# First tokens of the longer LSTMs in seven block products, and new places for the other stream's steps

## The chip, the cores and the metric

The kernel runs on one core of a Trainium2 chip. The time is the device time of one execution in microseconds (us), as a median over runs. The profile is one further execution, recorded instruction by instruction. TensorE is called PE here, VectorE DVE, ScalarE ACT, GpSimd POOL, and SyncE SP (in this kernel its queue issues nearly all DMAs). "L1155" is line 1155 of the kernel before.

## The reference, cut to what matters

Four residual layers work on x of 128 batches, 64 tokens and 256 channels in fp32. The change lies in layer 1: two graph convolutions, and then LSTMs over windows of p = 1, 2, 3 and 4 tokens, one after the other. Each overwrites the last token of each of its windows, so LSTM p+1 reads what LSTM p wrote.

```python
h = relu(adj @ (h @ Wg0 + bg0)); h = relu(adj @ (h @ Wg1 + bg1))
for p in range(1, 5):
    nw = 64 // p
    wins = h[:, :nw * p, :].reshape(128 * nw, p, 256)
    # per token: g = x_t @ Wih.T + h @ Whh.T + b; i, f, gg, o = split(g, 4)
    # c = sigmoid(f) * c + sigmoid(i) * tanh(gg); h = sigmoid(o) * tanh(c)
    last = lstm_last(Wih[p-1], Whh[p-1], bih[p-1], bhh[p-1], wins)
    h = h.at[:, arange(nw) * p + p - 1, :].set(last)
```

At a window's first token the state and the cell are zero. So only `x_t @ Wih.T` of the three gates i, gg and o is wanted there, and the cell is sigmoid(i) * tanh(gg).

## The kernel before, in words

**Tiling.** 512 rows of (batch, token) are a chunk; there are 16. Two chunks form a superchunk of 16 batches; there are eight, numbered 0 to 7. A superchunk lies in SBUF as `hT`: 128 partitions, two channel halves k, 64 tokens, 16 batches. The LSTM of p tokens has n = 16 * (64 // p) columns: 512, 336 and 256 for p = 2, 3, 4, and m = n/2.

**Seven block products.** A product of 256 by 256 weights with n columns is eight products of a 128x128 block with m columns. The kernel does it in seven (a Strassen-Winograd scheme). It needs sums of weight blocks, made once (`weight_sums`, L744) and reloaded per superchunk (`load_sets`, L883), sums of operands (`differences`, L309; `operands_x`, L1039, makes them for a token's input on POOL into an `xd` tile), and additions of the results. The class `Unit` (L1140) does this for one gate and one token. Kinds 1, 6, 7 and 4 fill bank x in turn, each on top of the last; kind 5 fills bank y; kinds 2 and 3 are two halves of bank z. Between them ACT copies a part out to `gates` (L1161) and DVE adds parts (L1164).

**The first token.** For p = 2, 3, 4 it is not done so. L1123 to L1128 are twelve plain products: three gates, two output halves, two input halves k, each n wide. Six with k = 0 come first, then a `yield`, then six with k = 1. ACT applies tanh or sigmoid straight from the banks (L1113), DVE makes the cell (L1119) and the state (L1093, `new_state`), and the operand sums of the state follow (`dh`, L313 to L316). Then come x products of token 1 for gates i and gg (kinds 5, 3 and 2: six of m columns), a `yield`, and token 1.

**Two streams.** All engines' queues are written in the order of the program. The LSTMs are a generator. Each `yield` is a mark n, counted from 0 in each superchunk; `yield "a"` is a half mark. In a superchunk the one-token LSTM ends at mark 3 and the others at 7, 13 and 21. At each mark the loop at the end runs the steps of the other stream due there, and they stand in every engine's queue at that place. Tuples name the marks:

- `convolutions` (15 steps a chunk) makes the next superchunk's `hT`: scaling; transposes and a trip through DRAM, with the load of xs; an addition (L284); statistics (L159, L160); two applies on ACT (L196); an aggregate on PE (L214); copies (L1005); products v (L915); bound (L921); products u (L929); bias (L935); a second aggregate; two ACT steps. `BEGUN` gives the first steps, a superchunk ahead, and `CONV` the rest (`FIRST` in superchunk 0).
- `residual` (three steps) puts the previous superchunk's `hT` back: transposes (L1277), loads, addition. Its tuple is `RESIDUAL`.
- `ahead` (six steps) prepares layer 2: a store and a reordering load, statistics, two applies, and transposes with a store (L272). Its tuples are `AHEAD` and `LATE`, and `FINAL` in the last superchunk.

Superchunk 7 has no convolutions. There `keep_busy` puts PE transposes at marks 5, 7, 9, 13 and 15.

**The end of an LSTM.** At its last token `new_state` writes `hT` in parts, the second channel half last (L1099; L1356 in the one-token LSTM), and then `ending` makes the operand sums for the next LSTM's token 1.

## Time and profile before

| what | value |
|---|---|
| time, median of 10 runs | 1877.54 us (1875.88 to 1879.07) |
| profiled execution, its own time | 1878.6 us |
| span in the profile, first to last instruction | 1876.8 us |
| mean granted PE clock | 0.998 of full |
| LSTM superchunks, first one-token product to the end of the last LSTM | 274 to some 1496 us |
| superchunk 3: LSTMs of 1, 2, 3, 4 tokens | 18.0, 42.7, 44.7, 49.2 us |
| PE idle in these | 0, 0, 0, 1.13 us |
| DVE busy in these | 13.2, 26.7, 29.5, 33.8 us |
| ACT busy in these | 14.9, 20.3, 25.3, 26.1 us |
| superchunk 7, the same four LSTMs | 18.0, 37.0, 43.9, 37.4 us |
| PE idle in these | 0, 0, 1.46, 1.87 us |

The page has parts: each engine's busy time, the span in slices, the DMA queues, the chain of work that ended last, and groups of instructions. A group has line, engine, operation, the names out<-in with shapes, a count, and then busy us and mean ns of one. The timeline lists instructions with start and duration in us; equal ones that follow each other are merged, and a bracket gives the idle time before and what ended it. A wide product appears as two passes, so the 288 products of L1126 count as 576.

### The profile page before, as it was taken

The page shows a single profiled execution, that of the slowest core. Times are in us where ns is not written, and L with a number is a line of the kernel's source. Part 1 is how long each engine was busy: PE and PEld are TensorE (multiplying, and loading weights), DVE is VectorE, ACT ScalarE, POOL GpSimd, SP SyncE. Part 2 cuts the span into 40 slices and gives each one's busy share as a digit, 9 for nine tenths or more (in the row PEclk, how much of TensorE's full clock was granted, in tenths as well). Part 3 has the DMA queues.
Part 4 walks back from the last instruction along what each step waited for, and adds up shares of the span by engine and source line. Part 5 has one row for each costly group of instructions (what it writes and reads, how often), then busy time and mean ns, then how long its engine had stood idle before and what let it go on. Part 6 is the DMA issues. An engine that isn't in the chain of part 4 may idle for free.

```text
span 1876.8 us, 39077 instructions
## 1 busy us (share of the span) xinstructions
PE 1848.0 (98%) x15077; PEld 1477.8 (79%) x15077; DVE 1245.2 (66%) x3150; ACT 1013.4 (54%) x2284; POOL 549.4 (29%) x704
## 2 busy tenths in 40 slices
PE   8999999999999999999999999999999999999998
PEld 6877856895897798699589689778968967777776
DVE  6768855566577666666666766666565567777776
ACT  5766635556456456555555645555565544444453
POOL 5855722122222212212222212222132113332232
PEclk9999999999999999999999999999999999999999
DMA  3223652134334433332433443343144254454433
GB/s 115 71 69 144 238 197 90 68 130 152 107 130 147 146 141 129 112 138 95 147 119 134 162 137 130 130 128 125 63 141 133 80 154 139 140 154 139 144 113 114
DMA packets 111274, 241.45 MB, mean 129 GB/s; under 512 B 11505, under 2 KB 74865, under 8 KB 111089
## 3 DMA queue, kind: packets, MB, share of 16 engines
q1 hardware_dynamic: 110192, 237.09, 37.5%
q8 instruction: 119, 1.95, 0.4%
q0 software_dynamic: 320, 1.05, 0.2%
q10 hardware_dynamic: 576, 0.82, 0.1%
q14 instruction: 67, 0.54, 0.1%
HBM read 170.50 MB, written 68.42 MB: 127 GB/s over the span
## 4 chain that ended last, share of the span: by engine, by line
PE 87%; DVE 6%; ACT 2%; DMA 2%; issue 1%; POOL 1%; SPq 0%; DVEq 0%; ACTq 0%
PE x L1155 21%; PE z L1155 10%; PE g L1126 9%; PE y L1155 5%; PE v L1580 5%; PE x L1340 4%; PE y L1340 3%; PE v L915 3%; PE u L929 3%; PE p_q L1587 3%; PE X L1776 3%; PE X L423 2%; PE X L499 2%; PE Y L1776 1%; PE Y L423 1%
## 5 line engine op out<-in xcount | busy, mean ns | idle before, releaser
L1155 PE MATMUL x<-xd,wset 128*128 128x128 f32 (+2 forms) x1152 | 256.9, 305 | 8.6 <-DVE gates L1164 8.5
L1155 PE MATMUL x<-hd,wset 128*128 128x128 f32 (+2 forms) x1152 | 255.3, 303 | 0.0
L1221 POOL TENSOR_TENSOR gates<-gates 128x512 f32<-128x512 f32 (+2 forms) x48 | 75.1, 1565 | 534.6 <-ACT gates L1084 534.6
L1084 ACT ACTIVATE gates<-gates,bias 128x256 f32<-128x256 f32 (+4 forms) x384 | 172.5, 488 | 103.7 <-DVE gates L1164 103.7
L1164 DVE TENSOR_TENSOR gates<-gates,x 128x128 f32<-128x128 f32 (+2 forms) x384 | 120.5, 321 | 145.2 <-PE x L1155 142.0
L1164 DVE TENSOR_TENSOR gates<-gates,z 128x128 f32<-128x128 f32 (+2 forms) x384 | 102.4, 318 | 150.2 <-PE z L1155 150.0
L1155 PEld LDWEIGHTS x<-xd,wset 128*128 128x128 f32 x1152 | 188.3, 192 | 16.6 <-DVE gates L1164 11.6
L1155 PEld LDWEIGHTS x<-hd,wset 128*128 128x128 f32 x1152 | 188.5, 192 | 5.0
L1126 PE MATMUL g<-hT,wset 128*128 128x256 f32 (+2 forms) x576 | 184.1, 474 | 0.1
L1126 PEld LDWEIGHTS g<-hT,wset 128*128 128x128 f32 x576 | 108.6, 190 | 68.1 <-issue 37.8
L1161 ACT COPY gates<-y 128x128 f32<-128x128 f32 (+2 forms) x192 | 53.9, 292 | 197.7 <-PE y L1155 195.9
L1155 PE MATMUL z<-hT,wset 128*128 128x128 f32 (+2 forms) x768 | 146.7, 303 | 0.0
L1155 PE MATMUL z<-hs,wset 128*128 128x128 f32 (+2 forms) x768 | 146.5, 303 | 0.2 <-DVE hs L1093 0.2
L1155 PEld LDWEIGHTS z<-hT,wset 128*128 128x128 f32 x768 | 117.2, 191 | 3.7
L1155 PEld LDWEIGHTS z<-hs,wset 128*128 128x128 f32 x768 | 117.2, 191 | 3.7 <-DVE hs L1093 0.3
L1113 ACT ACTIVATE gates<-g,bias 128x512 f32<-128x512 f32 (+2 forms) x144 | 74.9, 559 | 38.1 <-PE g L1126 37.5
L1084 ACT ACTIVATE gates<-x,bias 128x128 f32<-128x128 f32 (+2 forms) x192 | 74.8, 390 | 30.0 <-PE x L1155 27.6
L1155 PE MATMUL x<-hT,wset 128*128 128x128 f32 (+2 forms) x384 | 86.0, 306 | 0.2 <-ACT gates L1084 0.2
L1155 PE MATMUL x<-hs,wset 128*128 128x128 f32 (+2 forms) x384 | 84.9, 303 | 0.0
L1236 ACT ACTIVATE gates<-cell 128x256 f32<-128x256 f32 (+2 forms) x144 | 55.2, 383 | 48.4 <-DVE cell L1235 48.3
L1155 PE MATMUL y<-hd,wset 128*128 128x128 f32 (+2 forms) x384 | 79.7, 310 | 0.0
L1155 PE MATMUL y<-xd,wset 128*128 128x128 f32 (+2 forms) x384 | 77.5, 304 | 1.9 <-ACT gates L1113 1.9
(326 smaller groups left out, 4121.3 us busy)
## 6 DMA issues: line engine op xcount, KB each, us to landing
wset<-wfar SPq DMA_DIRECT2D x96, 960.0 KB, 6.5
hT<-far_h SPq DMA_DIRECT2D x124, 128.0 KB, 3.2
far_h<-hm SPq DMA_DIRECT2D x16, 512.0 KB, 2.8
far_n<-xs SPq DMA_DIRECT2D x16, 512.0 KB, 3.4
xs<-far_n SPq DMA_DIRECT2D x64, 128.0 KB, 4.1
far_x<-xs SPq DMA_DIRECT2D x16, 512.0 KB, 3.0
x<-far_x SPq DMA_DIRECT2D x64, 128.0 KB, 3.2
xt<-in_x_dram SPq DMA_DIRECT2D x15, 512.0 KB, 4.0
```

The lines of the kernel that those rows point to most:

```text
L423: nc.tensor.matmul(self.banks[tag][:, i * CH // 2 : (i + 1) * CH // 2], w, self.at[kind], start=first and not i, stop=True, skip_group_che ...
L915: nc.tensor.matmul(banks[m], wg0_sb[:, k, m * P : (m + 1) * P], agg[:, k, :], start=(k == 0), stop=(k == KD - 1))
L929: nc.tensor.matmul(banks[j // 2][:, j % 2, :], v[:, k, j * P : (j + 1) * P], wg1_sb[:, k, :], start=(k == 0), stop=(k == KD - 1))
L1084: nc.scalar.activation(gate(q, c, part), src, AF.Tanh if q == 2 else AF.Sigmoid, bias=bs[:, q * KD + c : q * KD + c + 1])
L1113: nc.scalar.activation(columns_of(gate(q, c)), natural(banks[q, c][:, :n].rearrange("p (w b) -> p w b", b=nb)), AF.Tanh if q == 2 else AF. ...
L1126: nc.tensor.matmul(banks[q, c][:, :n].rearrange("p (w b) -> p w b", b=nb), wsets[p, q][:, 2 * k + c, :], hv[:, k, : (nw - 1) * p + 1 : p, ...
L1155: nc.tensor.matmul(folded(self.psum(kind)), wsets[p, self.q][:, BLOCKS[kind][i], :], (ox[self.s] if part == "x" else oh)[kind], start=firs ...
L1164: nc.vector.tensor_add(gate(self.q, *dst), gate(self.q, *a), self.psum(kind))
L1221: nc.gpsimd.tensor_mul(gates[:, 0, :, :n], gates[:, 0, :, :n], gates[:, 2, :, :n])
L1340: nc.tensor.matmul(folded(ps(g, kind)), wih1[:, g, KINDS1[kind], :], right[kind], start=kind in (2, 5, 1), stop=True, skip_group_check=True)
L1580: nc.tensor.matmul(ps[:, i, :], hT[:, k, j, :], w[:, k, first : first + D], start=(k == 0), stop=(k == KD - 1))
L1776: nc.tensor.matmul(st[c, tag][:, i * CH // 2 : (i + 1) * CH // 2].rearrange("p (a n) -> p a n", n=P), w, st[c, "o7"][kind], start=first an ...
```

## The change

The first token of the two-, three- and four-token LSTMs becomes 21 products of m columns (class `First`): seven kinds for three gates. Copies, additions and acts come between them, and the biases stay in the acts. Gates i and gg take a bank of y and one of z each, gate o both of x. The marks within the first token change: the `yield` comes after kinds 1 and 5, and there is a new half mark (4.5, 8.5, 14.5) between the first and the second half of the state. Of token 1's x products only kinds 3 and 2 stay before the `yield`; kind 5 goes behind it. The input sums of the first token are made as well, so `xd` has three buffers. The weight set loses the one block that only the plain products used (15 to 14), and is stored in three pieces. The tuples of marks change. Without its empty lines, the diff is:

```diff
@@ -752,9 +752,9 @@
             for dst, a, b, op in ((4, 1, 3, OP.add), (5, 4, 0, OP.subtract), (6, 0, 1, OP.subtract),
                                   (7, 2, 5, OP.subtract)):
                 nc.gpsimd.tensor_tensor(v[:, :, dst], v[:, :, a], v[:, :, b], op)
-            far = dram.tile([P, 15, P], F32, tag=f"ws{p}{q}", name=f"wfar_{p}_{q}", bufs=1)
-            nc.sync.dma_start(far[:, :9], w[:, :9])
-            nc.sync.dma_start(far[:, 9:], w[:, 10:])
+            far = dram.tile([P, 14, P], F32, tag=f"ws{p}{q}", name=f"wfar_{p}_{q}", bufs=1)
+            for at, n, src in ((0, 1, 0), (1, 7, 2), (8, 6, 10)):
+                nc.sync.dma_start(far[:, at : at + n], w[:, src : src + n])
             wfar[p, q] = far
             yield
@@ -883,7 +883,7 @@
     def load_sets(n):
         for _ in range(min(n, len(coming))):
             p, q = coming.pop(0)
-            wsets[p, q] = w1.tile([P, 15, P], F32, tag="wset", name=f"wset_{p}_{q}", bufs=6)
+            wsets[p, q] = w1.tile([P, 14, P], F32, tag="wset", name=f"wset_{p}_{q}", bufs=6)
             nc.sync.dma_start(wsets[p, q], wfar[p, q])
@@ -1021,7 +1021,7 @@
-    BLOCKS = {1: (0, 8), 2: (2, 9), 3: (7, 14), 4: (3, 10), 5: (4, 11), 6: (5, 12), 7: (6, 13)}
+    BLOCKS = {1: (0, 7), 2: (1, 8), 3: (6, 13), 4: (2, 9), 5: (3, 10), 6: (4, 11), 7: (5, 12)}
     def columns_x(p, hv):
         nw, nb = hv.shape[2] // p, hv.shape[3]
@@ -1040,14 +1040,14 @@
         nw, nb, inner, tokens = columns_x(p, hv)
         m = nw * nb // 2
-        t = l1.tile([P, 7 * (T // 3) * NB], F32, tag="xd", name=f"xd_{name}_{s}", bufs=2)
+        t = l1.tile([P, 2 * CH], F32, tag="xd", name=f"xd_{name}_{s}", bufs=3)
         t = [t[:, i * m : (i + 1) * m].rearrange("p (a b) -> p a b", b=inner) for i in range(4)]
         b = {(k, j): tokens(k, s, j) for k in range(KD) for j in range(2)}
         for f in differences(nc.gpsimd, t, b[0, 0], b[0, 1], b[1, 0], b[1, 1]):
             f()
         return {5: t[0], 6: t[1], 7: t[2], 4: t[3], 1: b[0, 0], 2: b[1, 0], 3: b[1, 1]}
-    def lstm(p, hv, name, follows, x1, ending):
+    def lstm(p, hv, name, follows, ox, ending):
         nw, nb, inner, tokens = columns_x(p, hv)
@@ -1103,37 +1103,51 @@
         dh = differences(nc.vector, [hd[:, i, :m] for i in range(4)], b[0, 0], b[0, 1], b[1, 0], b[1, 1])
         oh = {i: folded(a) for i, a in {1: b[0, 0], 2: b[1, 0], 3: b[1, 1], 4: hd[:, 3, :m],
                                         5: hd[:, 0, :m], 6: hd[:, 1, :m], 7: hd[:, 2, :m]}.items()}
-        ox = {1: x1}
-
-        banks = {(q, c): bank(f"g{q}_{name}_{c}", tag) for q, tag in ((0, "y"), (2, "z"), (3, "x"))
-                 for c in range(KD)}
-        def first_acts(*qs):
-            for q in qs:
-                for c in range(KD):
-                    nc.scalar.activation(
-                        columns_of(gate(q, c)),
-                        natural(banks[q, c][:, :n].rearrange("p (w b) -> p w b", b=nb)),
-                        AF.Tanh if q == 2 else AF.Sigmoid, bias=bs[:, q * KD + c : q * KD + c + 1])
-
-        def first_cell(c):
-            nc.vector.tensor_mul(cells[:, c, :n], gate(0, c), gate(2, c))
-            nc.scalar.activation(gate(2, c), cells[:, c, :n], AF.Tanh)
-
-        products = [(q, c, k) for k in range(KD) for q in GATES[:3] for c in range(KD)]
-        for at, (q, c, k) in enumerate(products):
-            if at == 6:
-                yield
-            nc.tensor.matmul(
-                banks[q, c][:, :n].rearrange("p (w b) -> p w b", b=nb), wsets[p, q][:, 2 * k + c, :],
-                hv[:, k, : (nw - 1) * p + 1 : p, :], start=(k == 0), stop=(k == KD - 1))
-        first_acts(0, 2)
-        first_cell(0)
-        first_acts(3)
-        first_cell(1)
-        for c in range(KD):
-            new_state(0, c, every)
-            if not c:
-                dh[0]()
+
+        class First:
+
+            def __init__(self, q, tags):
+                self.q, self.ps = q, [bank(f"{t}{q}_{name}_{i}", t) for i, t in enumerate(tags)]
+
+            def psum(self, kind):
+                return self.ps[kind in (5, 3)][:, m:n] if kind in (2, 3) else self.ps[kind in (5, 3)][:, :m]
+
+            def product(self, kind):
+                nc.tensor.matmul(folded(self.psum(kind)), wsets[p, self.q][:, BLOCKS[kind][0], :], ox[0][kind],
+                                 start=kind in (1, 5), stop=True, skip_group_check=True)
+
+            def copy(self, c, j, kind):
+                nc.scalar.copy(gate(self.q, c, halves[j]), self.psum(kind))
+
+            def add(self, dst, a, kind):
+                nc.vector.tensor_add(gate(self.q, dst[0], halves[dst[1]]),
+                                     gate(self.q, a[0], halves[a[1]]), self.psum(kind))
+
+        firsts = [First(q, tags) for q, tags in ((0, "yz"), (2, "yz"), (3, "xx"))]
+
+        def all_first(*fs):
+            for f in fs:
+                for u in firsts:
+                    f(u)
+
+        def made(kind):
+            return lambda u: u.product(kind)
+
+        all_first(made(1), lambda u: u.copy(0, 0, 1), made(5), lambda u: u.copy(1, 1, 5))
+        yield
+        all_first(made(2), lambda u: u.add((0, 0), (0, 0), 2), made(3), made(6), lambda u: u.add((0, 1), (1, 1), 6),
+                  made(7), lambda u: u.add((1, 1), (1, 1), 7), lambda u: u.add((0, 1), (0, 1), 3), made(4),
+                  lambda u: act(u.q, 0, every, gate(u.q, 0)))
+        nc.vector.tensor_mul(cells[:, 0, :n], gate(0, 0), gate(2, 0))
+        nc.scalar.activation(gate(2, 0), cells[:, 0, :n], AF.Tanh)
+        all_first(lambda u: act(u.q, 1, halves[1], gate(u.q, 1, halves[1])),
+                  lambda u: act(u.q, 1, halves[0], u.psum(4)))
+        new_state(0, 0, every)
+        dh[0]()
+        yield "a"
+        nc.vector.tensor_mul(cells[:, 1, :n], gate(0, 1), gate(2, 1))
+        nc.scalar.activation(gate(2, 1), cells[:, 1, :n], AF.Tanh)
+        new_state(0, 1, every)
         dh[1]()
         dh[2]()
@@ -1201,14 +1215,14 @@
             return lambda u: getattr(u, f)(*a)
         A = [Unit(q, 1) for q in (0, 2)]
-        each(A, pe(5, "x"), pe(3, "x"), pe(2, "x"))
+        each(A, pe(3, "x"), pe(2, "x"))
         yield
         for s in range(1, p):
             last = s == p - 1
             B = [Unit(q, s) for q in (1, 3)]
             if not last:
                 ox[s + 1] = operands_x(p, hv, name, s + 1)
-            each(A, pe(5, "h"), do("copy", 5), pe(1), do("copy", 1), pe(3, "h"), pe(2, "h"), pe(6), do("u4"),
+            each(A, pe(5, "h" if s > 1 else "xh"), do("copy", 5), pe(1), do("copy", 1), pe(3, "h"), pe(2, "h"), pe(6), do("u4"),
                  do("c11"), do("c12"))
             each(B[:1], pe(5), do("copy", 5))
             each(A, pe(7), do("c22"), do("act", 0))
@@ -1301,9 +1315,8 @@
         t = []
         for i in range(2):
-            part = l1.tile([P, 7 * (T // 3) * NB], F32, tag="xd", name=f"xd_{name}_{i}", bufs=2)
-            for a in range(0, 2 * CH, CH):
-                v = part[:, a : a + CH]
+            part = l1.tile([P, 2 * CH], F32, tag="xd", name=f"xd_{name}_{i}", bufs=3)
+            for v in (part[:, :CH], part[:, CH:]):
                 wide = b[0, 0].shape[1:]
                 t.append(v.rearrange("p (a b) -> p a b", b=wide[1]) if len(wide) > 1 else v)
         a = b[0, 0], b[0, 1], b[1, 0], b[1, 1]
@@ -1420,7 +1433,7 @@
         def ending(p):
             if p < SKIP:
-                operands[p + 1] = operands_x(p + 1, hv, names[p + 1], 1)
+                operands[p + 1] = {s: operands_x(p + 1, hv, names[p + 1], s) for s in range(2)}
             elif sc < NCH // SUP - 1:
                 nxt = hTs[sc + 1].rearrange("p k (t b) -> p k t b", t=T)
                 operands[1] = block_sums(blocks(sc + 1, nxt), f"{sc + 1}_1")
@@ -1482,14 +1495,14 @@
-    RESIDUAL = (0, 3, 4), (2, 5, 5.5)
-    CONV = (3, 4, 4, 5, 5.5, 7, 8, 9, 10, 10), (3, 4, 4, 11, 11.5, 13, 14, 15, 15.5, 17, 18, 20)
-    BEGUN = (11, 11, 13, 14, 16), (17, 17.5, 19)
-    FIRST = (1, 2, 3, 3, 4, 4, 5, 5.5, 7, 8, 9, 10, 10), (3, 3, 5.5, 7, 8, 8, 11, 11.5, 13, 14, 15, 15.5, 17, 18, 20)
-    AHEAD = (4, 5, 7, 12, 14, 15), (6, 7)
-    LATE = 5, 6, 8, 9
+    RESIDUAL = (0, 3, 5.5), (2, 5, 8.5)
+    CONV = (3, 4, 5, 5.5, 7, 8, 9, 10, 10), (5, 6, 9.5, 11, 11.5, 13, 14, 15, 15.5, 17, 18, 20)
+    BEGUN = (11, 11, 14.5, 17, 19, 21), (17.5, 19, 21)
+    FIRST = (1, 2, 3, 3, 4, 4, 5, 5.5, 7, 8, 9, 10, 10), (1, 2, 4.5, 5, 6, 9.5, 11, 11.5, 13, 14, 15, 15.5, 17, 18, 20)
+    AHEAD = (6, 7), (9, 10)
+    LATE = (4.5, 5.5, 9, 9.5), (9, 11, 12, 19.5)
     IDLE = {5: 4, 7: 18, 9: 10, 13: 14, 15: 8}
-    FINAL = (4, 5, 10, 12, 12, 14), (6, 7, 11, 14, 14, 16)
+    FINAL = (6, 7, 11, 12, 15, 15.5), (9, 10, 15, 16, 17, 17.5)
     START = (0, 1, 0, 0, 0, 1, 0, 1, 1, 0, 0, 1, 1, 0, 1, 2, 2)
     tc.no_sync_barrier()
@@ -1526,8 +1539,6 @@
                     todo.setdefault(n, []).append(unit)
-            if sc > 1:
-                units(LATE[:1], aheads[sc * SUP - 3])
             if sc < last:
                 for i in range(SUP):
                     units((CONV if sc else FIRST)[i], convs[(sc + 1) * SUP + i])
@@ -1538,7 +1549,8 @@
             else:
                 units([0], convs[1])
             if sc > 1:
-                units(LATE[1:], aheads[sc * SUP - 3])
+                for i in range(SUP):
+                    units(LATE[i], aheads[(sc - 2) * SUP + i])
             if sc:
                 for i in range(SUP):
                     units((FINAL if sc == last else AHEAD)[i], aheads[(sc - 1) * SUP + i])
```

## The prediction

> **What bounds the kernel now.** I read the page first: busy shares, then the chain of work that ended last.

> ```profile
> PE 1848.0 (98%) x15077; PEld 1477.8 (79%) x15077; DVE 1245.2 (66%) x3150; ACT 1013.4 (54%) x2284; POOL 549.4 (29%) x704
> PE 87%; DVE 6%; ACT 2%; DMA 2%; issue 1%; POOL 1%; SPq 0%; DVEq 0%; ACTq 0%
> ```

> TensorE (PE) is the bound: it idles for 29 us of 1876.8. A product saved is time saved, if PE has no new wait; a wait of PE costs its whole length. So everything below is counted on PE's queue. What does one product cost? The groups of instructions, shapes kept apart (busy us, mean ns), show each fp32 product as two passes:

> ```profile
> L1126 PE MATMUL g<-hT,wset 128*128 128x512 f32 x192 | 85.6, 596 | 0.0
> L1126 PE MATMUL g<-hT,wset 128*128 128x336 f32 x192 | 55.6, 447 | 0.0
> L1126 PE MATMUL g<-hT,wset 128*128 128x256 f32 x192 | 42.9, 380 | 0.1
> ```

> The mean is a latency. From start to start, passes that follow each other in the timeline are 0.429, 0.283, 0.216 us apart at 512, 336, 256 columns, and in the blocked products of L1155 0.216, 0.143, 0.112 us at 256, 168, 128: half the columns, about half the time. Then I read the timeline at the three first tokens of one superchunk (start, duration), here the three-token LSTM, PE alone:

> ```profile
> 801.19 6.94 PE L1126 MATMUL g<-hT,wset 128*128 128x336 f32 x24
> 807.97 0.73 PE L1155 MATMUL y<-xd,wset 128*128 128x168 f32 x4
> 808.54 1.30 PE L1155 MATMUL z<-hT,wset 128*128 128x168 f32 x8
> 809.77 1.16 PE L214 MATMUL agg_c<-adjt_bd,cv 64*64 64x64 f32 x64
> ```

> No gap: the x products and the other stream's L214 hide the gates' chain (acts, cell, state, L313), and token 1 follows at 810.87. Last, PE's longer gaps in this stage. A recurring one:

> ```profile
> 885.88 1.29 DVE L284 TENSOR_TENSOR xs<-xs,cv 128x512 f32<-128x512 f32 x2 [1.11 <-DMA xs<-in_x_dram]
> 887.43 0.49 PE L1155 MATMUL x<-xd,wset 128*128 128x128 f32 x2 [0.90 <-DVE gates L1164]
> ```

> VectorE (DVE) stands in its queue before a DMA, and PE behind it. Such gaps are 0.64, 1.30, 1.06, 2.74 us in superchunks 0, 2, 3, 5 (5.7 us); one of 0.40 us at 40 to 50% of the four-token LSTM comes in superchunks 0 to 5.

> [...] L1356 takes 0.68 us, but 1.19 us where POOL's L314 runs. [...]

> **The change, part by part.**

> *Products.* Per superchunk 12 of n columns go, 24 x (0.429+0.283+0.216) = 22.3 us; 21 of n/2 come, 42 x (0.216+0.143+0.112) = 19.8 us. That is 2.5 us, over 8 superchunks 19.9 us, if nothing waits.

> *DVE, ACT, POOL, DMA work.* Per LSTM 12 adds (steps 0.33, 0.24, 0.20 us): 9 us more of DVE per superchunk of some 155 us, of which it is busy 103. ACT: six copies, and nine acts for six, about 7 us more. POOL: four differences more, 0.4 to 0.7 us each. None is PE time; they cost only where PE stands behind one, which the walks below count. Weight sets shrink from 960 to 896 KB; they land some 15 to 40 us before use. Twelve more DMA issues in the weight stage lie behind PE's work there: nothing. SP's moved puts stand before weight loads with that same slack: nothing; without it, up to the landing of 6.5 us once per LSTM. The third xd buffer adds no wait.

> *Two-token LSTM (T=758.54, PE's first product).* Its last operand comes late:

> ```profile
> 758.54 5.31 PE L1126 MATMUL g<-hT,wset 128*128 128x512 f32 x12
> 761.42 1.19 DVE L1356 TENSOR_TENSOR hT<-cell,gates 128x512 f32<-128x512 f32 x1 [0.17 <-ACT gates L1353]
> ```

> Before, six wide products covered it. After: L214 is moved ahead (1.1 us), six narrow products (2.6) end at T+3.7; the copies into the gates start only after the state at T+4.07, copy 0.37 and 0.2 of handing over, so product 2 starts at T+4.63: 0.9 us of PE wait. Fifteen products (6.5), four x products (1.7), L915 (3.4) and the two x products moved behind it (0.9) bring T+17.1. Before, 776.15-758.54 = 17.6. **-0.5 us.** L915 is the cover here: the bank that token 1 needs is free 3.9 us after product 4, at T+15.0, against T+16.3.

> *Three-token LSTM (T=801.19).* State at T+1.27, so product 2 waits 0.1. Product 7 waits for DVE's add of 6, and 4 for that of 7: product to add 0.55, add 0.33, back 0.16, against three products of 0.29: 0.17 each. Product 4 ends at T+6.45; x products 1.15 and L214 1.1: PE is at token 1 at T+8.7. Token 1's first bank is the one that product 4 filled, and ACT reads it only fourth after the tanh of cell 0: product 4 + 3.2 = T+9.65, with the way back T+9.75. That is 1.05 us, because only L214 (not a long L915 or L929) lies there. With the moved x products (0.57) T+10.3, against 9.7: +0.6. Behind it the h products wait 0.2 for the second state, since a residual sum (1.2 us of DVE) now stands ahead of it at mark 8.5. From superchunk 2 on 2.1 us of statistics at mark 9 stand ahead of token 1's adds (before: squares of 1.4): 0.6. **+0.8, from superchunk 2 on +1.4 us.**

> *Four-token LSTM (T=845.90).* 21 products 4.7, adds' pace 0.26 twice, x products 0.9, L929 3.45, moved x products 0.45: T+10.02 against 9.98. **0.0.** L929 covers the chain; without it the bank comes 2.8 us after product 4 and 1.9 us show. At marks 17 and 19 the moved statistics (2.1) and transposes (1.4) cost PE 0.2 each: **+0.4** in superchunks 0 to 5.

> *What the moves take away.* The conv input loaded at 17.5 and added at 19 is now loaded at 19 and added at 21: the DMA gap goes, 5.7 us; the apply at 16 goes, and with it 0.40 six times, 2.4 us.

> *First superchunk.* The aggregate at mark 4 waits for both applies: +1.0 in the two-token LSTM; the 1.27 us that acts of the three-token LSTM stood behind an apply go. With the rest 0.0.

> *Last superchunk.* No other stream covers, only short idle transposes, and its two-token LSTM waits still longer for its operand:

> ```profile
> 1381.47 1.19 DVE L1356 TENSOR_TENSOR hT<-cell,gates 128x512 f32<-128x512 f32 x1 [0.16 <-ACT gates L1353]
> ```

> From T=1377.72: state at T+4.94, product 2 at 5.5, product 4 ends at 12.0, bank at 15.9, moved x products: 16.7 against 13.3, +3.4. Three tokens: state T+2.67, product 4 at 7.8, bank 11.1: 11.7 against 9.7, +2.0. Four: +0.9. Gaps of 1.46 and 0.91 behind misplaced steps go: **+3.9 us.**

> *Sum.* Superchunks 2 to 6: 5 x (-0.5+1.4+0.0) + 4 x 0.4 - 5.1 - 1.6 = -0.6; superchunk 1: -0.5+0.8+0.4-0.4 = +0.3; 0: 0.0; 7: +3.9. Together some +4 us: a span of 1881, a run of 1882.5 beside the profiled one (1878.6, 1.8 above its span and 1.1 above the median), against the median **1882 us**. So of 19.9 us nothing is left; some 32 us of first-token waits and work behind take it, less 8 us of waits removed.

> **Rivals.**
> *Faster, 1869.* The one mechanism: the y bank in the three-token LSTM. If ACT frees it 1.1 us earlier, and DVE's statistics end in time, 1.85 us go from seven superchunks, 13 us. For it: ACT is only 57% busy in that LSTM (25.3 of 44.7 us). Against: the four acts and the tanh stand in a fixed order.
> *No change, 1878.* The last superchunk costs nothing net: its cover is short, but so were the gaps there.
> *Much slower, 1892.* DVE falls behind: marks 4.5, 8.5, 14.5 put 1.3 to 2.1 us before the second cell, and each of 24 first tokens loses 0.4 us more. Against: DVE is idle a third of the stage.
> That the change doesn't do what it says is excluded: the built program's queue has 21 products per first token.

> **How the numbers follow.** Forecast 0.38, faster 0.25, no change 0.25, much slower 0.12. Within 0.2% (3.8 us, about what a measurement of this kernel can tell from no change) is the third; slower is forecast and last, 0.50. Unknown in size are the bank-grained waits: from nothing (two bank waits gone, -13) to half a microsecond more at each first token (+12). Range 1868 to 1893; the forecast's own is 1879 to 1887.

> **What would show it.** Right: a PE gap of about 1 us before the first y product of token 1 in the three-token LSTM, put down to ACT; 0.9 us before product 2 in the two-token one; the L284 DMA gap gone; a last superchunk longer by 4 us. Wrong: first tokens without gaps (then 2.5 us per superchunk are gained), or gaps where the moved steps stand instead.

## The result, and the profile after

The changed kernel takes **1896.66 us** (median, 1895.88 to 1897.86), against 1877.64 before (median of 28 runs): a ratio of 1.0102, 95% interval 1.0093 to 1.0111. The forecast was 1882 us, with a range of 1868 to 1893. It is slower, as forecast, but by 19 us where 4 were counted, and outside the range.

The page of the kernel after, engine totals and the chain of work that ended last:

```profile
PE 1838.8 (97%) x15509; PEld 1513.8 (80%) x15509; DVE 1325.1 (70%) x3438; ACT 1053.2 (56%) x2500; POOL 599.1 (32%) x800
PE 79%; DVE 11%; ACT 5%; issue 2%; POOL 2%; DMA 1%; SPq 0%; ACTq 0%; DVEq 0%; POOLq 0%
```

PE was busy for 1848.0 of 1876.8 us; now it is for 1838.8 of 1895.7. The products did become cheaper, and PE's idle time went from 29 to 57 us. On the chain, DVE and ACT have 16% where they had 8% before. DVE works 80 us more; 9 us of that per superchunk are the additions that were counted.

So the question is where PE stands. The groups of instructions, shapes kept apart for the first line (busy us, mean ns, then PE's idle time ahead of the group and what ended it), give two places at once:

```profile
L1116 PE MATMUL y<-hT,wset 128*128 128x256 f32 x64 | 17.9, 402 | 4.8 <-ACT gates L1120 4.8
L1169 PE MATMUL x<-xd,wset 128*128 128x128 f32 (+2 forms) x1152 | 256.6, 304 | 12.3 <-ACT gates L1175 10.1
```

L1116 is the first token's product (L1120 its copy), and that wait was foreseen. L1169 is the later tokens' product (L1155 before), L1175 their copy (L1161 before). Its group stood for 8.6 us before, behind DVE. Now ACT's copies hold it for 10.1 us, and no step of the prediction has that.

The stretches of the timeline, from the first product of an LSTM to the first of the next (for the very last one, to its last product), say in which superchunk and LSTM the time lies (us; superchunk 4 is a typical one):

| | before | after | predicted | measured |
|---|---|---|---|---|
| up to the first superchunk | 274.0 | 274.7 | 0 | +0.7 |
| superchunk 0 | 157.98 | 160.80 | 0.0 | +2.8 |
| superchunk 1 | 153.71 | 155.01 | +0.3 | +1.3 |
| superchunks 2 to 6, sum | 774.0 | 776.2 | -0.6 | +2.1 |
| of these, superchunk 4: p = 1 and 2 | 60.68 | 60.27 | -0.5 | -0.4 |
| p = 3 | 44.71 | 45.96 | +1.4 | +1.25 |
| p = 4 | 48.30 | 49.24 | 0.0 | +0.9 |
| superchunk 7 | 146.33 | 153.33 | +3.9 | +7.0 |
| after the last LSTM | 370.8 | 375.8 | 0 | +5.0 |

The measured column adds up to 18.9 us, the difference of the spans. (The last LSTM of the kernel before ends at 1506.0 us. The table ahead of the prediction stopped at 1496, so it gives its four-token LSTM 10 us too little.)

The four waits that make up most of it, each in its timeline (start, duration; the bracket is the idle time ahead). First the four-token LSTM of superchunk 4, before the last token, DVE, ACT and PE together:

```profile
1045.95 0.15 DVE L194 SCALAR_TENSOR_TENSOR nmr_b<-mv_b,rstd_b 128x4 f32<-128x4 f32 x1
1046.14 1.09 ACT L196 ACTIVATE cv<-xs,nmr_b,rstd_b 128x256 f32<-128x256 f32 x2 [1.09 <-DVE nmr_b L194]
1047.14 0.41 ACT L1175 COPY gates<-y 128x128 f32<-128x128 f32 x2
1047.86 0.35 PE L1169 MATMUL x<-xd,wset 128*128 128x128 f32 x1 [1.40 <-ACT gates L1175]
```

The moved apply (L196, mark 19) stands at the head of ACT's queue. It waits for a small DVE operation (L194), which stands behind the end of the token before. The copies of the last token stand behind the apply, and PE behind the copies. From start to start PE loses 1.56 us here, in superchunks 0 to 4 alike, and 1.91 us in superchunk 5: 9.7 us.

Second, the two-token LSTM of superchunk 0:

```profile
296.78 0.23 POOL L99 TENSOR_SCALAR rstd_b<-mv_b 128x4 f32<-128x4 f32 x1 [4.23 <-DVE mv_b L160]
297.10 1.04 POOL L100 TENSOR_TENSOR rstd_b<-rstd_b,mhalf 128x4 f32<-128x4 f32 x1
298.11 0.95 POOL L313 TENSOR_TENSOR xd<-hT 128x256 f32<-128x256 f32 x1
299.11 1.00 PE L1116 MATMUL z<-xd,wset 128*128 128x256 f32 x2 [2.25 <-POOL xd L313]
```

Product 5 of the first token needs POOL's difference of the operand. POOL had stood idle for 4.23 us, waiting for DVE's statistics (L160): the square root of the other stream that needs them (L99, L100) stands ahead of the difference in POOL's queue. Before, the first token read the plain operand and needed no POOL.

Third, after the last LSTM, SP's queue (its DMA issues) and then PE:

```profile
1488.36 27.16 SPq L247 DMA_DIRECT2D far_n<-nm  x3
1515.58 0.42 SPq L1581 DMA_DIRECT2D wqv_sb<-wqv_far  x1
...
1522.43 1.96 PE L1599 MATMUL p_q<-hT,wqv_sb 128*128 128x512 f32 x4 [2.21 <-DMA wqv_sb<-wqv_far]
```

The weights of the next stage are issued at 1515.58 because three stores stand ahead, the last of them in place at mark 19.5. Before, that load was issued at 1478.6, 27 us ahead of its use. PE loses 2.4 us from start to start.

Fourth, what was predicted: a wait of 0.88 us in the three-token LSTM, before token 1, behind ACT (L1084), and one of 0.72 us from start to start before product 2 in the two-token one (0.56 us in the bracket), behind ACT's copy out of the other half of its bank (L1120):

```profile
923.61 0.65 ACT L1120 COPY gates<-y 128x256 f32<-128x256 f32 x2 [1.39 <-DVE hT L1369]
924.03 1.13 PE L1116 MATMUL y<-hT,wset 128*128 128x256 f32 x4 [0.56 <-ACT gates L1120]
...
969.37 1.16 PE L214 MATMUL agg_c<-adjt_bd,cv 64*64 64x64 f32 x64
971.41 0.52 PE L1169 MATMUL y<-xd,wset 128*128 128x168 f32 x2 [0.88 <-ACT gates L1084]
```

### The profile page after: what moved, and what is told of

Its sections match the earlier page's. It is cut to its first block, busy times and chain, and to the rows that moved or that the text cites. A ratio compares the mean times of both kernels' runs of the same rounds, so it can differ in the third digit from the quotient of the medians.

```text
span 1895.7 us, 40708 instructions
## 1 busy us (share of the span) xinstructions
PE 1838.8 (97%) x15509; PEld 1513.8 (80%) x15509; DVE 1325.1 (70%) x3438; ACT 1053.2 (56%) x2500; POOL 599.1 (32%) x800
## 3 DMA queue, kind: packets, MB, share of 16 engines
q0 software_dynamic: 320, 1.05, 0.2%
## 4 chain that ended last, share of the span: by engine, by line
PE 79%; DVE 11%; ACT 5%; issue 2%; POOL 2%; DMA 1%; SPq 0%; ACTq 0%; DVEq 0%; POOLq 0%
PE x L1169 20%; PE z L1169 10%; PE v L1592 5%; PE y L1169 5%; PE y L1116 4%; PE u L929 3%; PE v L915 3%; PE p_q L1599 3%; PE y L1353 3%; PE X L1788 3%; PE x L1353 2%; PE X L423 2%; PE x L1116 2%; PE X L499 2%; PE z L1116 1%
## 5 line engine op out<-in xcount | busy, mean ns | idle before, releaser
L1084 ACT ACTIVATE gates<-gates,bias 128x256 f32<-128x256 f32 (+4 forms) x528 | 237.7, 495 | 203.9 <-DVE gates L1178 108.9
L1169 PE MATMUL x<-xd,wset 128*128 128x128 f32 (+2 forms) x1152 | 256.6, 304 | 12.3 <-ACT gates L1175 10.1
L1169 PE MATMUL x<-hd,wset 128*128 128x128 f32 (+2 forms) x1152 | 254.5, 303 | 0.0
L1169 PEld LDWEIGHTS x<-xd,wset 128*128 128x128 f32 x1152 | 187.3, 191 | 21.5 <-issue 11.5
L1169 PEld LDWEIGHTS x<-hd,wset 128*128 128x128 f32 x1152 | 187.8, 191 | 5.0
L1169 PE MATMUL z<-hs,wset 128*128 128x128 f32 (+2 forms) x768 | 146.3, 303 | 0.0
L1169 PE MATMUL z<-hT,wset 128*128 128x128 f32 (+2 forms) x768 | 146.2, 303 | 0.0
L1175 ACT COPY gates<-y 128x128 f32<-128x128 f32 (+2 forms) x192 | 53.0, 289 | 131.9 <-PE y L1169 125.6
L1169 PEld LDWEIGHTS z<-hs,wset 128*128 128x128 f32 x768 | 116.9, 191 | 3.6 <-DVE hs L1093 0.3
L1169 PEld LDWEIGHTS z<-hT,wset 128*128 128x128 f32 x768 | 117.1, 191 | 3.3
L1084 ACT ACTIVATE gates<-x,bias 128x128 f32<-128x128 f32 (+2 forms) x216 | 84.5, 391 | 31.5 <-PE x L1169 28.3
L1169 PE MATMUL y<-xd,wset 128*128 128x128 f32 (+2 forms) x384 | 81.7, 305 | 9.8 <-ACT gates L1084 9.8
L1169 PE MATMUL x<-hT,wset 128*128 128x128 f32 (+2 forms) x384 | 85.8, 305 | 0.0
L1169 PE MATMUL x<-hs,wset 128*128 128x128 f32 (+2 forms) x384 | 84.8, 303 | 0.0
L1169 PE MATMUL y<-hd,wset 128*128 128x128 f32 (+2 forms) x384 | 82.5, 307 | 0.0
L313 POOL TENSOR_TENSOR xd<-hT 128x128 f32<-128x128 f32 (+2 forms) x72 | 41.9, 582 | 128.2 <-DVE hT L1095 105.7
L1607 POOL TENSOR_TENSOR s<-s,mx 128x256 f32<-128x256 f32 (+2 forms) x33 | 40.4, 1225 | 132.1 <-DVE mx L1606 124.3
L1594 ACT COPY v<-v 128x512 f32<-128x512 f32 x64 | 37.1, 581 | 72.6 <-PE v L1592 72.5
```

Of the source, the lines that this page charges most:

```text
L1084: nc.scalar.activation(gate(q, c, part), src, AF.Tanh if q == 2 else AF.Sigmoid, bias=bs[:, q * KD + c : q * KD + c + 1])
L1169: nc.tensor.matmul(folded(self.psum(kind)), wsets[p, self.q][:, BLOCKS[kind][i], :], (ox[self.s] if part == "x" else oh)[kind], start=firs ...
```

## The experiments

Times are medians. Each group was run beside the kernel before, which took 1876.93, 1876.73 and 1877.91 us in the three groups.

**Each half of the change alone.** `products_alone` keeps the block products and takes back the places:

```diff
-    RESIDUAL = (0, 3, 5.5), (2, 5, 8.5)
-    CONV = (3, 4, 5, 5.5, 7, 8, 9, 10, 10), (5, 6, 9.5, 11, 11.5, ...
+    RESIDUAL = (0, 3, 4), (2, 5, 5.5)
+    CONV = (3, 4, 4, 5, 5.5, 7, 8, 9, 10, 10), (3, 4, 4, 11, 11.5, ...
...  (BEGUN, FIRST, AHEAD, LATE, FINAL and the loop that hands LATE out likewise)
```

> The seven block products with the places of the steps as they were before. Theory (both halves of the change cost, through different waits): the two-token LSTM gains 0.4 us and the three-token one loses 0.6 to 0.9 us in superchunks 1 to 6, the last superchunk loses about 7 us, the wait for the late input (1 to 2.7 us in four superchunks) and the 0.40 us wait come back, the 1.56 us wait in the last token and the 2.4 us weight wait after the last superchunk are gone: 1884 to 1888 us. Rival 1 (the products carry the loss): 1893 to 1898 us. Rival 2 (the places carry it): 1875 to 1879 us.

`places_alone` keeps the twelve wide products, with the new places and a `yield "a"` between the two halves of the first token's state.

> The twelve wide products as before, with the new places of the steps. Theory: a wait of about 1.56 us before the last token of the four-token LSTM in superchunks 0 to 5 (9.7 us together) and one of 2.4 us or more for the weights after the last superchunk; the waits for the late input and the 0.40 us waits are gone (some 9 us); 1879 to 1884 us. Rival 1 (the products carry the loss): 1868 to 1877 us. Rival 2 (the places carry it): 1890 us or more.

| | old places | new places |
|---|---|---|
| twelve wide products | 1876.9 | 1878.6 (1.0007, 0.9999 to 1.0016) |
| seven block products | 1970.8 (1.0502, 1.0487 to 1.0516) | 1896.7 |

All three expectations missed for the block products at the old places: they cost 94 us, where the theory had 7 to 11 and its dearest rival 21. The wide products at the new places came 0.4 us under the theory's range. The two halves are not a sum. The new places by themselves change nothing that a measurement tells, and with the block products they are worth 74 us. The two-token LSTM of superchunk 2 shows why (timeline of `products_alone`, DVE, POOL and PE):

```profile
636.59 1.04 POOL L100 TENSOR_TENSOR rstd_b<-rstd_b,mhalf 128x4 f32<-128x4 f32 x1
637.66 0.16 DVE L194 SCALAR_TENSOR_TENSOR nmr_b<-mv_b,rstd_b 128x4 f32<-128x4 f32 x1 [2.31 <-POOL rstd_b L100]
637.84 1.29 DVE L284 TENSOR_TENSOR xs<-xs,hT 128x512 f32<-128x512 f32 x2
639.05 0.75 DVE L1123 TENSOR_TENSOR gates<-gates,y 128x256 f32<-128x256 f32 x2
639.61 2.05 PE L1116 MATMUL y<-xd,wset 128*128 128x256 f32 x4 [4.21 <-DVE gates L1123]
```

The block products need DVE in the middle of the first token (L1123), and they put eight differences on POOL where there were four. The apply step at mark 4 has a small DVE operation (L194), which waits for POOL's square root (L100), and that stands behind those eight. The residual sum (L284) comes next on DVE, and only then the additions for which PE waits. The wide products needed neither engine until they were done.

After such waits PE is slow too: the next product starts 1.84 us after these four passes (at 641.45), 0.46 us for each where 0.216 was normal. The granted PE clock of that stretch (columns: window, its length, then busy us of PE, PEld, DVE, ACT, POOL, and the clock):

```profile
639.50:641.50 2.00, 1.89 (x5) 1.57 (x6) 1.05 (x3) 0.44 (x1) 0.00 (x0) 0.50 0.77 265
641.50:643.50 2.00, 2.00 (x6) 1.64 (x5) 0.94 (x3) 0.00 (x0) 0.00 (x0) 0.50 1.02 245
```

**Is it the idleness?** Idle transposes were put into PE's gap. In the first try they came one product late, and so after the gap:

```diff
+        def fill():
+            return [lambda u: u.q == 0 and keep_busy(28, f"f{name}")]   # p == 2, superchunks 0 to 6
-                  made(7), lambda u: u.add((1, 1), (1, 1), 7), ...
+                  *fill(), made(7), lambda u: u.add((1, 1), (1, 1), 7), ...
```

> The seven block products with the old places (1970.8 us measured), with 28 idle transposes on TensorE put before product 7 of the two-token LSTM in superchunks 0 to 6, where TensorE stood for 4.2 us and then ran at a granted clock of 0.50. Theory (the half clock after the wait is caused by the idleness itself and costs some 2.9 us each time): the wait for VectorE's add stays, the passes after it run at full clock: 1948 to 1956 us. Rival (those passes are slow for what VectorE and the DMA do at that time): 1968 to 1976 us.

It took 1990.99 us, since the filling ran inside the slow stretch and was added to it. The second try put the same call between `made(3)` and `made(6)`, at the head of the gap.

> As the run with idle transposes, which put them one product too late (they came after the wait, inside the slow stretch, and added 3 us to each two-token LSTM). Now they stand before product 6, at the head of TensorE's 4.37 us gap of superchunks 1 to 6. Theory (the half clock is caused by TensorE's idleness): the passes after the gap run at full clock and each of six or seven two-token LSTMs takes some 2.5 to 3 us less than with the block products alone at the old places (48.4 to 49.2 us): 1949 to 1957 us against 1970.8. Rival (the slow passes come from what the other engines and the DMA do): 1968 to 1976 us.

It took 1960.04 us, 10.8 below `products_alone`. The wait stays, the slow passes are gone (PE, and the clock of the same stretch):

```profile
635.00 3.22 PE L151 MATMUL idle_f<-ident 128*128 128x128 f32 x28
639.39 1.10 PE L1116 MATMUL y<-xd,wset 128*128 128x256 f32 x4 [1.16 <-DVE gates L1123]
```

```profile
639.50:641.50 2.00, 2.00 (x10) 1.54 (x10) 1.72 (x6) 0.21 (x1) 0.00 (x0) 1.00 0.83 286
641.50:643.50 2.00, 2.00 (x11) 1.73 (x10) 1.98 (x6) 0.46 (x1) 0.00 (x0) 1.00 0.88 235
```

The two-token LSTM falls from 48.4 to 49.2 us to 46.7 in superchunks 1 to 5 and to 47.0 in superchunk 6, by 1.4 to 2.5 us each. In `products_alone` all six of these gaps were followed by the half clock, here none, with DVE and the DMA as busy as before: the mechanism is as expected. The time missed the expected range, 1949 to 1957 us, by 3 us, for two reasons. The two-token LSTM of superchunk 0 rose by 3.1 us: it had no such gap, and there the filling is pure cost. And the profiled execution (1953.3 us) was the fastest of the four, with a mean clock of 0.998 where the others had 0.991 to 0.993; it gained another 6 us in the four-token LSTMs, where nothing was filled. There the same wait of 2.73 us was followed by the half clock five times of six in `products_alone` and never here; the last section shows what decides that.

**Which places matter to the block products.** `conv_places` is `products_alone` with `CONV` and `BEGUN` alone as the change has them.

> The seven block products with the old places, except the next superchunk's convolution steps, which stand where the change has them. Theory (an apply in the two-token LSTM's first token, and statistics in the four-token one's, wait for GpSimd behind its eight differences, with VectorE's adds queued behind them): the two-token LSTM falls from 48.4 to 49.2 us to some 42, the four-token one from 53.4 to some 49, some 60 us together: 1900 to 1915 us. Rival (the residual sums and the ahead steps in the first tokens hold VectorE): over 1940 us.

It took 1932.87 us: 38 of the 74 us, between theory and rival. The four-token LSTM fell to 49.24 us as the theory said. The two-token one fell only to 43.8 to 45.4, and the row that holds it in superchunk 4 (DVE) is the rival's:

```profile
944.79 2.12 DVE L284 TENSOR_TENSOR xs<-xs,hT 128x512 f32<-128x512 f32 x2 [1.84 <-DMA hT<-far_h]
946.83 0.74 DVE L1123 TENSOR_TENSOR gates<-gates,y 128x256 f32<-128x256 f32 x2
```

The residual sum at mark 4 waits for its load with the additions behind it. Both kinds of step had to leave the first tokens.

**The apply at mark 19.** `apply20` moves one number of the changed kernel:

```diff
-    BEGUN = (11, 11, 14.5, 17, 19, 21), (17.5, 19, 21)
+    BEGUN = (11, 11, 14.5, 17, 20, 21), (17.5, 19, 21)
```

> The changed kernel; the first apply of the next superchunk's first convolution goes from mark 19, between two tokens, to mark 20, inside the last token. Theory (ScalarE's apply stands ahead of the copies that TensorE needs): the 1.56 us wait goes from superchunks 0 to 5, at most 0.4 us each is left: 1887 to 1890 us. Rival (VectorE's transposes at mark 19 or the statistics before it hold the copies up): the wait stays, 1895 to 1897 us.

It took 1886.69 us, 10.0 us less than the changed kernel. The four-token LSTM falls from 49.24 to 47.60 us in superchunk 4, and DVE's transposes at mark 19 stayed where they were. The place of the apply in ACT's queue is the cause.

**The bank of product 4.** `bank_first` swaps the last two rows of acts in the first token:

```diff
-        all_first(lambda u: act(u.q, 1, halves[1], gate(u.q, 1, halves[1])),
-                  lambda u: act(u.q, 1, halves[0], u.psum(4)))
+        all_first(lambda u: act(u.q, 1, halves[0], u.psum(4)),
+                  lambda u: act(u.q, 1, halves[1], gate(u.q, 1, halves[1])))
```

> The changed kernel; of the last six activations of each first token, the three that read the banks of product 4 now come before the three that read SBUF. Theory (PE's wait before token 1 is for those banks): the 0.88 us wait in the three-token LSTM and the 1.95, 1.08 and 1.11 us waits of the last superchunk shrink by up to 0.9 us each: 1887 to 1890 us. Rival (the whole chain up to the second state is the limit, so the wait reappears before the h products): 1895 to 1897 us.

It took 1895.74 us, as the rival said. In the three-token LSTM of superchunk 4 the wait before token 1 is gone, and PE stands eight products later, behind the second state:

```profile
971.21 0.45 PE L1169 MATMUL x<-hs,wset 128*128 128x168 f32 x2
972.07 1.12 PE L1169 MATMUL z<-hs,wset 128*128 128x168 f32 x6 [0.42 <-DVE hs L1093]
```

The LSTM takes 45.97 us as before. The bank was only the first thing to be late; the length of the chain from product 4 through acts, cell, tanh and state sets the time. The residual sum that now stands at mark 8.5 is part of that chain: in superchunk 0, which has none, the same swap shortened the three-token LSTM from 45.31 to 44.84 us.

**The other two waits.** `places3` has the apply at 20, and

```diff
-    FIRST = (1, 2, 3, 3, 4, ...
+    FIRST = (1, 1, 3, 3, 4, ...
-    FINAL = (6, 7, 11, 12, 15, 15.5), (9, 10, 15, 16, 17, 17.5)
+    FINAL = (6, 7, 11, 12, 15, 15.5), (9, 10, 12, 15.5, 16, 16)
```

> The changed kernel with three steps placed anew: the apply of mark 19 at mark 20 (alone 1886.7 us measured), the statistics of the second superchunk's first convolution at mark 1 in place of 2 in the first superchunk, and in the last one the statistics, applies and put of the second chunk at 12, 15.5, 16, 16 in place of 15, 16, 17, 17.5. Theory: the 2.4 us wait for GpSimd's difference in the first superchunk goes, with the half clock after it (3 us together), and so does the wait for the weights behind the last put (1 to 2.4 us): 1881 to 1884 us. Rival (the waits only pass to the next instruction in these queues): 1886 to 1888 us.

It took 1887.9 us; the rival held. With the statistics at mark 1, PE's wait for POOL's difference goes, and a new one of 2.51 us stands in the one-token LSTM, whose additions are behind the statistics on DVE: +2.24 and -2.34 us. In the last superchunk the applies at their new marks cost 1.2 us. The weights still came late, for the last of the three stores was not one of `FINAL`'s but `LATE`'s, at mark 19.5. `late16` moves that one, in superchunk 7 only:

```diff
+    EARLY = (4.5, 5.5, 9, 9.5), (9, 11, 12, 16)
-                    units(LATE[i], aheads[(sc - 2) * SUP + i])
+                    units((LATE if sc < last else EARLY)[i], aheads[(sc - 2) * SUP + i])
```

> The changed kernel with the apply at mark 20 (1886.7 us measured), and in the last superchunk the late put, whose place was 19.5, at 16. Theory (the load of the next stage's weights stands behind that put in SP's queue): the weights are there in time, the stretch after the last LSTM shrinks by 1 to 2.4 us: 1884 to 1886 us. Rival (another put, or the transfer itself, is late): 1886.5 to 1888 us.

The load is issued 17.0 us before PE is done with the last LSTM (1492.66 against 1509.7), where it was 4.4 in the changed kernel, and PE's wait for it is gone. Yet the kernel takes 1887.19 us: the four-token LSTM of superchunk 7 is 0.94 us longer with that step at mark 16. The cause of the wait is settled; moving it bought nothing.

**A kernel that takes only what pays.** In `mix` the block products stand in the two-token LSTM of superchunks 1 to 6 alone, all else as in `places3` with wide products; `mixwide` has none.

```diff
+    def SEVEN(name):
+        return name[-1] == "2" and name[0] in "123456"   # mixwide: False
...
+        if seven:
+            (class First and its order, as in the changed kernel)
+        else:
+            (the twelve products, with the half mark after the first state)
```

> Places as in the kernel with three new places; seven block products only in the two-token LSTM of superchunks 1 to 6, where they gained 0.41 us each, twelve wide products elsewhere. Theory (with the places right, the products cost only where nothing covers the chain of the first token): wide products with the new places took 1878.6, less 9.7 for the apply, less some 2 for the weights, less 6 x 0.41: 1863 to 1867 us, below both kernels. Rival (the places cost as much elsewhere): 1874 us or more.

> As the mixed kernel, with twelve wide products everywhere. Theory: 2.5 us above the mixed kernel, 1865.5 to 1869.5 us. Rival (the block products give nothing in the two-token LSTM): the same time as the mixed kernel, within 0.5 us.

They took 1869.4 and 1868.89 us. Both beat the kernel before (0.9961, 0.9948 to 0.9973, for `mix`); `mix` lies between its theory and its rival, and between the two kernels there is nothing that a measurement tells, as the rival of `mixwide` said. The block products do gain 0.41 us in each of the six two-token LSTMs (41.05 against 41.46 us), 2.5 us together. In the profiled executions two things eat it: in superchunk 0, where the two kernels' work is the same, the same wait of 2.51 us was followed by the half clock in `mix` and not in `mixwide`, 1.65 us, and the stretch after the last LSTM is 1.1 us longer in `mix`. But other executions of `mix` ran at a mean clock of 1.000, took 1869.1 to 1869.4 us, and were no faster than those of `mixwide`. So where the 2.5 us go there is not shown.

`best` is `mix` without what `places3` had wrong (`FIRST` begins 1, 2 and `FINAL` is as in the change); the second tuple of `FIRST` begins 3, 3, 5.5, 6, 7, and `EARLY = (4.5, 5.5, 9, 9.5), (9, 11.5, 12, 16)`.

> Block products in the two-token LSTM of superchunks 1 to 6 only, apply at mark 20, the late put of the last superchunk at 16 and its apply at 11.5 in place of 11, the first superchunk's second convolution begun at 3, 3, 5.5, 6, 7 and the rest as in the changed kernel. Theory: against the mixed kernel (1869.4) 3 us less in the first superchunk, 2.5 to 4 in the last one and 1 to 2 at the weights: 1860 to 1864 us. Rival (these waits pass on): 1867 us or more.

It took **1865.86 us**, between theory and rival, a ratio to the kernel before of 0.9935 (0.9922 to 0.9949):

```profile
PE 1838.7 (99%) x15185; PEld 1494.1 (80%) x15185; DVE 1270.3 (68%) x3222; ACT 1023.3 (55%) x2338; POOL 564.3 (30%) x728
PE 89%; DVE 6%; ACT 2%; issue 1%; POOL 1%; DMA 1%; SPq 0%; DVEq 0%; ACTq 0%
```

PE's idle time is 26 us, less than before, with PE's own work 9 us smaller. Against `mix` the first superchunk takes 2.5 us less, of which 1.65 were the half clock, and the last one 2.1. The gain over the kernel before comes from the places: its waits for the late input are gone, and the apply doesn't stand ahead of the copies. `mixwide`, with no block products at all, already has 0.9961. `best` with wide products everywhere was not run, so it is open whether its block products give anything.

## Why the prediction was wrong, step by step

**What held.** The two-token LSTM: -0.5 predicted, -0.4 measured, with the wait before product 2 of 0.9 predicted (an estimate: no row of before had such a wait) and 0.72 measured. The three-token LSTM: +0.8, and +1.4 from superchunk 2 on; measured +0.61 and +1.25, with the wait put down to ACT as said. The late input's gaps went as forecast. So did the sign for being wrong that the prediction named last, gaps where the moved steps stand instead: that is what the traces show. The block products' part in superchunks 1 to 6 was sized within 0.2 us in each of these two LSTMs.

**The failing step: "What the moves take away".** It says that the apply at mark 16 goes, and with it 0.40 us six times. The apply doesn't go; it stands at mark 19, and there it costs PE 1.56 us in five superchunks and 1.91 in the sixth. "At marks 17 and 19" priced the statistics and the transposes that DVE gets there, and never asked what stands behind the apply on ACT. With the apply inside a token instead, 10.0 us of the 15 us missed are gone (`apply20`). What was priced, 0.4 us for statistics and transposes, cost nothing: with them and the apply at mark 20 the four-token LSTM takes 47.60 us, and in superchunk 6, which has neither, 47.72. The prediction's own row at 885.88 shows such a stand: DVE idle for 1.11 us before a DMA, and PE for 0.90 us behind it. The rows of L196 and L1175 show the same of ACT: idle for 1.09 us until L194 is done, the copies behind the apply, and PE idle for 1.40 us. The queues were walked so for the new first token and not for the moved step.

**"First superchunk ... the rest 0.0".** The aggregate that waits for both applies was priced at +1.0; with wide products it is +1.36 (`places_alone`, 44.73 against 43.37 us). The queue of POOL was not walked: 2.41 us for the difference behind the square root. The half clock after it cost little there: `late16`, whose program is that of `apply20` up to the last superchunk, has the same wait without it and takes 46.04 us for this LSTM, against 46.48. Measured +2.8, of which 1.56 is the apply at mark 19.

**"SP's moved puts ... nothing".** It named the price without cover ("up to the landing of 6.5 us"), and took the cover of the middle superchunks for granted at the end of the last one, where the next stage's load is behind the puts. That is 2.4 of the 5.0 us after the last LSTM. Two gaps of 0.67 us at L1867 there (0.8 to 0.9 us each with what follows) come with nothing that the profile shows as their cause. They are absent with wide products everywhere, and one such gap is in `mix` and in `best`; they stay open. A last 0.8 us lies behind PE's last instruction and was not followed up.

**The last superchunk, +3.9.** The moves gain 2.6 us there with wide products, near the 2.4 predicted, but by luck: an apply at mark 11, between two tokens of the three-token LSTM, stands ahead of the copies in the same way as the one at mark 19 and costs PE 1.38 us, in the changed kernel and in `places_alone`. With it at 11.5 (`best`) that wait is gone. The block products cost 3.96, 2.75 and 2.88 us in its three LSTMs (after less `places_alone`), where 3.4, 2.0 and 0.9 were taken. The term most wrong is the four-token LSTM: the text gave 1.9 us for a first token without L929, and the sum used 0.9.

**"Gaps of 5.7 us".** In superchunk 5 the removal was worth more than the 2.74 us of the gap. In the kernel before, PE ran at half clock for 3.4 us after it, from 1197.8 to 1201.2 (window, length, busy us, and the clock as a mean over each window):

```profile
1197.40:1199.00 1.60, 1.58 (x9) 1.59 (x10) 1.23 (x6) 0.82 (x2) 0.00 (x0) 0.62 0.00 0
1199.00:1203.00 4.00, 4.00 (x28) 4.00 (x28) 0.29 (x1) 1.91 (x8) 0.30 (x1) 0.73 0.26 65
```

Its four-token LSTM took 52.53 us where superchunk 4's took 48.30: 2.73 us of gap and 1.5 us of slow passes. So a part of the miss is hidden: without the wait behind the apply, superchunks 2 to 6 gained 4.1 us (`apply20` against before) where the prediction had 0.6.

**The rivals.** The time came nearest to "much slower, 1892", but not by its mechanism: the half marks cost the three-token LSTM what was predicted and no more. "Faster, 1869" rested on the y bank alone. `bank_first` shows that freeing the bank gives nothing in superchunks 1 to 7, since the second state is late next. "No change" asked for a last superchunk without cost; it cost 7 us. No rival was about a moved step in the later tokens, and the range did not reach it.

## What to carry to other kernels

A step that was moved cost what stood behind it in an engine's queue at the new place: 1.56 us behind an apply on ACT, 2.4 us behind a square root on POOL, 2.4 us behind stores on SP. So walk the queues of ACT, DVE, POOL and SP at a step's new place one by one, and put it inside a token where PE has products in hand, not between two. Splitting one long run of products into short ones with copies and additions between them made PE depend here on engines that it had left alone, so the neighbours' steps had to be moved first; that was worth 74 us. Where the saving is a few tenths per use, ask whether it reaches the total: six times 0.41 us showed in the LSTMs of `mix` and not in its time.

## What the runs showed of the hardware that was not expected

A wait of PE could cost more than its length: after some waits PE ran at half clock (in the kernel before for 3.41 us after one of 2.74 us), and where the filling kept it off, 1.4 to 2.5 us were gained each time. Of the waits in the LSTM stage of all fourteen traces, with the idle time in the bracket as the measure, all 16 of 3.6 us or more were followed by the half clock, 25 of 40 between 2.24 and 2.74 us, and none of the 12 between 1.75 and 2.21 us.

```profile
289.94:293.35 3.41, 1.13 (x3) 0.19 (x1) 3.41 (x8) 1.83 (x3) 2.03 (x3) 1.00 0.00 0
293.35:296.77 3.42, 3.35 (x4) 1.51 (x5) 2.99 (x6) 3.26 (x7) 1.89 (x2) 0.50 0.00 0
```

In `mixwide` it is split between two:

```profile
289.21:292.62 3.41, 1.95 (x5) 0.57 (x3) 3.34 (x9) 1.02 (x2) 1.61 (x2) 1.00 0.00 0
292.62:296.04 3.42, 2.53 (x6) 1.24 (x7) 2.99 (x6) 3.26 (x6) 1.50 (x2) 1.00 0.00 0
296.04:299.45 3.41, 3.41 (x9) 1.52 (x8) 2.88 (x6) 3.01 (x6) 0.84 (x1) 1.00 0.32 132
```

In the stage before the LSTMs, with other products, the half clock came now and then after 1.1 to 1.4 us of idle time in a step (in the kernel before after 1.39 us, in the step that ends at 252.28 us), so the figure of 2.05 us is this stage's. The step need not be idle throughout: 2.05 of its 3.41 us were enough in these runs. And filling helped where it left less than that: in `keepbusy2` 1.16 us of the wait in superchunk 2 were left, and the clock stayed at 1.00.
